# Twelve-layer decoder on one core: first keys and values of layers two and eight projected in the layers before them, statistics and transposes of layer five moved, orders of DVE in layer nine joined

## The chip, the cores and the metric

One program runs on one core of a Trainium2 chip. The core has a TensorE (PE, matrix products and transposes), a VectorE (DVE), a ScalarE (ACT), a GpSimdE (POOL) and a queue for transfers (SP), each with an instruction stream of its own. Semaphores order the streams, and what waits in a stream holds everything behind it. The metric is the device time of one execution in microseconds: 3483.48 us, the median of three runs (3479.71 to 3483.94).

## The reference

Eight sequences of 256 positions with 256 channels go through four decoder layers of three sublayers each, so twelve steps, which are here called layers one to twelve. (The code counts them from 0: layer one is `l0_attn`, named 0 in tiles and pools, and layer nine is `l2_ffn`, named 8.) After each sublayer a layer norm follows:

```python
x = _layernorm(x + _L0_attn_ref(x, ...))              # one: 16 heads of 16
x = _layernorm(x + _L0_xattn_ref(x, ctx_768, ...))    # two: one head of 256, keys from a context
x = _layernorm(x + _L0_ffn_ref(x, ...))               # three: all of 8 experts
x = _layernorm(x + _L1_attn_ref(x, ...))              # four: 16 heads, biases linear in distance
x = _layernorm(x + _L1_xattn_ref(ctx_768, x, mask_BxS2_bk0, ...))  # five: keys from both
x = _layernorm(x + _L1_ffn_ref(x, ...))               # six: 2 of 8 experts for a whole sequence
x = _layernorm(x + _L2_attn_ref(x, ...))              # seven: 16 heads, causal
x = _layernorm(x + _L2_xattn_ref(x, ctx_768, ...))    # eight: 8 heads of 64 over the context
x = _layernorm(x + _L2_ffn_ref(x, ...))               # nine: below
...                                                   # ten, eleven: 16 heads of 64; twelve: experts
```

In layer nine a shared expert (squared ReLU) works on every token. Of eight routed experts the best two by a router count with the integer part of their softmax weight, which is 0 unless one weight rounds to 1:

```python
prob = jnp.trunc(prob)
h = _sq_relu(jnp.einsum('td,edf->tef', xf, W1))
out_routed = jnp.einsum('ted,te->td', y, prob)
return (out_shared + out_routed).reshape(shape)
```

## The kernel before

All is float32. The activations of a sequence (an element, b = 0 to 7) lie in `xs[b]`, positions on partitions, and transposed in `xT`, two elements to a tile. The layers are unrolled one behind the other.

**What sets the order.** The program is written as text, and a planner lays down each engine's instructions before the run: it goes through time with a cost model and gives each engine the earliest instruction in the text that is ready by then, so work of a later layer can come before the end of an earlier one. Tiles come from pools with a number of buffers, and a tile waits for the release of the buffer that it gets. A pool's memory is free once every tile in it has been read for the last time. Weights come from a ring of six tiles (`wtile`), loads by SP; a load can go as soon as its ring tile is free. Where the planner's order is not wanted, `order_of_text` (L161) chains the instructions of the engines it names in the order of the text. Only what goes through `matmul`, `transpose`, `dve` and `pool` is chained (L149); `nc.vector`, `nc.scalar` and `nc.gpsimd` are not. `behind_latest` (L140) ties an unchained stretch behind the latest recorded instruction.

**Evacuation.** `evac` (L183) copies from PSUM by a counter, every third copy on ACT and the others on DVE. `leave` (L190) takes ACT where DVE is chained, without counting, and `evac` elsewhere.

**16-head layers** (one, four, seven; `attention16`, L390) chain PE and DVE. A block i is half the heads of an element, so block 14 and 15 are the last element. It has four steps: `step` (L466) forms scores of block i + 1 for their maxima (DVE), scores of block i, transposed and with the maxima subtracted, and their exponential (ACT). Between the steps stand the projections of the next element, the products with the values (`attend`), the normalisation (`normalise`, two reciprocals and two products on DVE), the output projection of the element before and its norm. In the last element no projections of a next one stand between the steps.

**Layer two** (`l0_xattn`, L1000) has no chain: for each element queries (`pq`), keys (`pk`), values (`pv`), scores, softmax, products and norm.

**Layers eight, ten, eleven** (`attention64`, L688) chain PE alone. Two units (pairs of heads) share a group's projections; a unit's scores, its exponentials and their transposition, and its products with the values go in a pipeline three units deep.

**Layer five** (`l1_xattn`, L1143) chains PE and DVE. For element b the four stages `front_sources`, `front_project`, `front_values`, `front_heads` run beside the four units of the element before. `front_stats` and `front_norms` precede them. The statistics of element 0 (`begin4`, L1131) are formed at the end of layer four. `finish` transposes a finished element. `choose` (L1365) finds the two experts of layer six for element 0 in the middle of layer five, 25 small DVE instructions on a path of their own.

**Layer nine** (`l2_ffn`, L1480). For each of four pairs of elements the router is computed: logits (`token_logits`, L865: product, copy `lT`, transpose, copy `L`), the best two (`top2`), softmax, gates. The last element's norm and transpose are left over from layer eight (`left`, three parts) and are worked off ahead of the fourth pair. Then the gates are summed over all tokens (`most`, `count`). A branch on the count skips the routed experts where it is 0. `expert(p, 0)` is the shared expert of pair p: product `ph`, ReLU on ACT, square on DVE, product `py`, addition. After the branch come the fourth shared expert and the norms of elements 0 and 1.

## Time and profile before

The profiled execution took 3468.22 us, of which the span is 3466.5 us. By stretches of the span (engine columns: us busy):

| stretch, us | what | length | PE | DVE | ACT | POOL | granted clock |
|---|---|---|---|---|---|---|---|
| 0 to 236 | layer one | 236 | 216.37 | 155.17 | 102.06 | 22.87 | 0.99 |
| 236 to 322 | layer two | 86 | 82.33 | 44.77 | 17.36 | 7.41 | 1.00 |
| 985 to 1216 | layer four | 231 | 214.96 | 178.19 | 67.26 | 21.05 | 0.98 |
| 1216 to 1236 | layer five, start | 20 | 14.60 | 11.74 | 7.37 | 15.64 | 0.83 |
| 1236 to 1450 | layer five, rest | 214 | 199.22 | 145.86 | 126.82 | 155.52 | 0.98 |
| 1676 to 1906 | layer seven | 230 | 203.42 | 177.60 | 83.88 | 59.31 | 0.96 |
| 1906 to 2136 | layer eight, begin of nine | 230 | 218.46 | 124.51 | 87.52 | 77.37 | 1.00 |
| 2136 to 2165 | layer nine, rest | 29 | 15.68 | 15.61 | 2.08 | 2.78 | 0.71 |

A row of the timeline gives start, duration, engine, line, operation, the tile written and those read, their shapes, and in brackets how long the engine was idle before and what ended that. Most lines of `matmul` are L178, of `transpose` L181 and of `dve` L173, so a row is known by its tiles. The granted clock is the share of full speed that TensorE got.

### The profile page before, as it was taken

Reading aid. Unit: us, or ns where it says so; the run is one execution under the profiler, and the core shown is the slowest. Engines: PE = TensorE matmul, PEld = TensorE weight load, DVE = VectorE, ACT = ScalarE, POOL = GpSimd, SP = SyncE. Lnnn points to the kernel's source line nnn. Section 1 sums busy time; section 2 is a strip of 40 time slices with the busy share of each in tenths; the row PEclk is TensorE's granted clock in tenths of the full one; section 3 lists DMA queues with packets and bytes.
Section 4 is the critical chain, followed back from the end, with each engine's and each line's share of the span. In section 5 each row is a group of like instructions: output and inputs, shape, how many; then the busy total and the mean of one; then the engine's idle time right before and its main releaser. Section 6 shows DMA issues by size and latency. Waiting matters only on the chain. (4 is left out here: it accounts for less than half of the span.)

```text
span 3466.5 us, 49726 instructions
## 1 busy us (share of the span) xinstructions
PE 3291.9 (95%) x20456; PEld 2353.2 (68%) x20456; DVE 1657.3 (48%) x3181; ACT 1057.8 (31%) x2563; POOL 849.8 (25%) x918
## 2 busy tenths in 40 slices
PE   8999999999999989999898998999998999999998
PEld 5666555655555566788666665677776766678887
DVE  5764222222358777521587555766665455530003
ACT  4432111111113355522333342433333443321111
POOL 1000000000011077522122332332223344332214
PEclk9999999999999999999999999999999999999999
DMA  3006400000000001144100101000000000025542
GB/s 107 2 10 138 173 19 19 19 19 25 22 1 1 2 13 57 55 166 156 51 2 2 49 1 56 7 1 1 1 14 30 1 13 13 13 88 190 187 147 76
DMA packets 63386, 168.35 MB, mean 49 GB/s; under 512 B 7888, under 2 KB 38353, under 8 KB 51441
## 3 DMA queue, kind: packets, MB, share of 16 engines
q1 hardware_dynamic: 47408, 76.15, 7.4%
q0 software_dynamic: 15744, 88.94, 7.2%
q8 instruction: 165, 2.70, 0.3%
q14 instruction: 69, 0.56, 0.1%
HBM read 131.78 MB, written 33.29 MB: 48 GB/s over the span
## 5 line engine op out<-in xcount | busy, mean ns | idle before, releaser
L670 POOL TENSOR_TENSOR ex<-ex,urc 128x1024 f32<-128x1024 f32 x192 | 363.4, 1894 | 615.7 <-DVE urc L173 581.4
L173 DVE TENSOR_REDUCE nm<-s 128x4 f32<-128x1024 f32 (+2 forms) x448 | 455.7, 1030 | 100.1 <-PE s L178 49.4
L661 ACT ACTIVATE ex<-s,nm 128x256 f32<-128x256 f32 (+1 forms) x704 | 337.7, 493 | 390.8 <-DVE nm L173 371.2
L515 ACT ACTIVATE eT<-t 128x1024 f32<-128x1024 f32 (+1 forms) x192 | 182.7, 953 | 353.1 <-PE t L178 353.1
L1097 DVE TENSOR_TENSOR h<-pu,sg 128x512 f32<-128x512 f32 x128 | 88.5, 691 | 331.3 <-PE pu L933 326.4
L1096 ACT ACTIVATE sg<-pg 128x512 f32<-128x512 f32 x128 | 76.3, 597 | 548.9 <-PE pg L933 548.8
L933 PE MATMUL pu<-xT_l,w2a 128*128 128x512 f32 x512 | 241.3, 593 | 0.0
L933 PE MATMUL pg<-xT_l,w2a 128*128 128x512 f32 x512 | 241.3, 593 | 0.0
L178 PE MATMUL s<-qk,qk 32*128 32x256 f32 (+1 forms) x1536 | 212.9, 393 | 25.8 <-DVE nm L173 18.8
L918 PE MATMUL py<-w2b,h 128*128 128x256 f32 x1024 | 226.2, 379 | 0.0
L918 PEld LDWEIGHTS py<-w2b,h 128*128 128x128 f32 x1024 | 195.0, 190 | 39.6 <-issue 15.3
L181 PE MATMUL etr<-ident,ex 128*128 128x128 f32 x1568 | 210.5, 277 | 7.3 <-POOL ex L670 2.4
L178 PE MATMUL t<-qm,qk 32*128 32x256 f32 (+1 forms) x1536 | 204.0, 386 | 8.5 <-DVE nm L173 7.2
L181 PEld LDWEIGHTS etr<-ident,ex 128*128 128x128 f32 x1568 | 176.6, 141 | 51.7 <-issue 34.4
L178 PE MATMUL av<-eT,vg 128*64 128x256 f32 x1536 | 204.7, 391 | 0.7 <-DVE eT L173 0.6
L178 PE MATMUL s<-kg,qg 64*128 64x256 f32 x1280 | 176.8, 395 | 26.3 <-ACT qg L732 12.1
L178 PEld LDWEIGHTS s<-qk,qk 32*128 32x128 f32 x1536 | 123.6, 187 | 92.6 <-issue 46.7
L933 PEld LDWEIGHTS pu<-xT_l,w2a 128*128 128x128 f32 x512 | 97.2, 191 | 120.7 <-issue 120.2
L933 PEld LDWEIGHTS pg<-xT_l,w2a 128*128 128x128 f32 x512 | 96.7, 190 | 106.1 <-issue 104.7
L178 PEld LDWEIGHTS s<-kg,qg 64*128 64x128 f32 x1280 | 115.2, 186 | 77.8 <-ACT qg L732 26.5
L173 DVE COPY eT<-etr 128x1024 f32<-128x1024 f32 (+1 forms) x113 | 134.6, 1191 | 57.9 <-PE etr L181 57.8
L173 POOL TENSOR_SCALAR ve_l<-mv_l 128x2 f32<-128x2 f32 x104 | 23.5, 226 | 532.2 <-DVE mv_l L173 531.4
(351 smaller groups left out, 5878.3 us busy)
## 6 DMA issues: line engine op xcount, KB each, us to landing
slots<-zero SPq DMA_DIRECT2D x16, 1024.0 KB, 13.0
given<-yo SPq DMA_DIRECT2D x19, 256.0 KB, 3.1
w2a<-in_L_ffn_Wg SPq DMA_DIRECT2D x8, 512.0 KB, 4.1
w2a<-in_L_ffn_Wu SPq DMA_DIRECT2D x8, 512.0 KB, 4.9
w2b<-in_L_ffn_Wd SPq DMA_DIRECT2D x8, 512.0 KB, 3.9
lines<-w9r SPq DMA_DIRECT2D x1, 4096.0 KB, 42.7
bias<-lines SPq DMA_DIRECT2D x4, 768.0 KB, 8.9
x<-in_x SPq DMA_DIRECT2D x8, 256.0 KB, 5.4
```

What stands on the lines that cost most here:

```text
L173: return lambda *args, **kw: in_order(getattr(getattr(nc, self.engine), op)(*args, **kw))
L178: in_order(nc.tensor.matmul(*args, **kw))
L181: in_order(nc.tensor.transpose(*args))
L515: nc.scalar.activation(eT[:, :, :n], tt[:, :, :n], AF.Exp)
L661: nc.scalar.activation(ex[:, g, :], flat[:, g, :], AF.Exp, bias=nm[:, g:g + 1], accum_out=sums[:, g:g + 1])
L670: nc.gpsimd.tensor_tensor(ex, ex, rc[:, :nseg].unsqueeze(2).to_broadcast([P, nseg, 1024 // nseg]), ALU.mult)
L918: nc.tensor.matmul(py[:, q * D:(q + 1) * D], h[:, f, i * P:(i + 1) * P], w2[:, f, :], start=(f == 0), stop=(f == nf - 1))
L933: nc.tensor.matmul(ph, w1[:, c, f * P:(f + 1) * P], xT[p][:, c, :], start=(c == 0), stop=(c == 1))
L1096: nc.scalar.activation(sg, pg, AF.Silu)
L1097: nc.vector.tensor_tensor(h[:, f, :], pu, sg, ALU.mult)
```

## The change

- Layer one loads layer two's weights in its own text (`prepare1`) and computes the keys and values of element 0 between steps 0, 1 and 2 of block 14 (`fill`), into a ring tile. Layer two takes them for element 0. The key bias of element 0 goes on ACT; the value bias is recorded in DVE's chain.
- Layer seven does the same for layer eight's first group (`begin`, `end`), evacuated by ACT.
- `at_end` (layer five's first statistics) moves from behind block 15's normalisation to behind block 14's. Element 1's statistics move behind element 0's sources. The transposes of the last two elements in layer five move to later units.
- `choose(0, 1)` in layer five leaves DVE's chain (`free_order`).
- Layer nine chains DVE. The last element's norm comes first, the logits of all pairs go into one tile, and one best-of-two over all 16 token blocks (`choose8`) replaces four. An expert is split into its two halves.
- Helpers of routers and experts record their DVE instructions, and `iota8` has one row of eight.

```diff
-    iota8 = const.tile([P, 4, E8], F32, tag="iota8", name="iota8")
-    nc.gpsimd.iota(iota8, pattern=[[0, 4], [1, E8]], base=0, channel_multiplier=0,
+    iota8 = const.tile([P, 1, E8], F32, tag="iota8", name="iota8")
+    nc.gpsimd.iota(iota8, pattern=[[0, 1], [1, E8]], base=0, channel_multiplier=0,
...
+    @contextmanager
+    def free_order(engine):
+        last = chains.pop(engine)
+        yield
+        chains[engine] = last
...
                             pk = project_qk(b + 1, 1)
+                        else:
+                            work_off(fill, 1)
                         step(i, 1)
+                        if not more:
+                            work_off(fill, 1)
...
                             pv = proj_tok(wv, xTb(b + 1), 0, f"pv_{li}_{b + 1}")
+                        elif at_end is not None:
+                            at_end()
...
-                if at_end is not None:
-                    at_end()
...
             parts = project(*units[0][:2])
-            for i in (3, 0, 1, 2):
+            if kv is not None:
+                groups[0, 0].update(k=kv[0], v=kv[1])
+            for i in (3, 0, 1, 2) if kv is None else (3,):
                 parts[i]()
...
     def top2(L, n, name):
+        for got in top2_parts(L, n, name):
+            pass
+        return got
+    def top2_parts(L, n, name, small=small):
...
+            yield vals, hots, ids
...
+    def token_logits(xTp, wr, name, pool, L=None):
...
-        nc.vector.tensor_copy(lT, pl[:, 0:P])
+        dve.tensor_copy(lT, pl[:, 0:P])
...
+            dst = L
+            if dst is None:
+                dst = small.tile([P, 2 * NT, E8], F32, tag="L", name=f"L_{name}")
+            dve.tensor_copy(dst, tr[:, 0:P].rearrange("p (i e) -> p i e", e=32)[:, :, :E8])
+            return dst
...
-    def top2_gates(p, wr, gates, name, trunc, pool):
...
-                nc.vector.tensor_tensor(xs[b], py.rearrange("p (q d) -> p q d", q=NT), xs[b],
+                dve.tensor_tensor(xs[b], py.rearrange("p (q d) -> p q d", q=NT), xs[b],
...
+        fill = []
+        if not last:
+            prepare1()
+            ready1["kv"] = first_keys(1)
+            fill = [lambda: keys1(ready1["kv"][0], 0), lambda: values1(ready1["kv"][1], 0)]
...
+                    bv=bv, bo=bo, last=last, arrive=arrive, fill=fill)
...
-    def l0_xattn(last):
+    ready1 = {}
+    def prepare1():
...
+        ready1["w"] = wq, wk_, wv, halves, bqs, bk, bv
+    def keys1(dst, b):
+        _, wk_, _, halves, _, bk, _ = ready1["w"]
+        pk = proj_T(wk_, [h[:, b * S:(b + 1) * S] for h in halves], 0, f"pk_1_{b}")
+        for c in range(2):
+            if b == 0:
+                nc.scalar.activation(dst[:, c, :], pk[:, c * S:(c + 1) * S], AF.Identity,
+                                     bias=bk[:, c:c + 1])
+            else:
+                nc.vector.tensor_scalar(dst[:, c, :], pk[:, c * S:(c + 1) * S], bk[:, c:c + 1],
+                                        None, ALU.add)
+    def values1(dst, b):
+        _, _, wv, halves, _, _, bv = ready1["w"]
+        pv = proj_tok(wv, [h[:, b * S:(b + 1) * S] for h in halves], 0, f"pv_1_{b}")
+        dve.tensor_tensor(dst, pv.rearrange("p (q d) -> p q d", q=NT),
+                          bv.unsqueeze(1).to_broadcast([P, NT, D]), ALU.add)
+    def first_keys(name):
+        w = wtile(f"kv{name}")
+        return [w[:, 512 * i:512 * i + 512].rearrange("p (c s) -> p c s", c=2) for i in range(2)]
+    def l0_xattn(last):
+        if not ready1:
+            prepare1()
+        wq, _, _, _, bqs, _, _ = ready1["w"]
...
-                pk = proj_T(wk_, kv, 0, f"pk_{nm}")
...
-                pv = proj_tok(wv, kv, 0, f"pv_{nm}")
...
+                if b == 0 and "kv" in ready1:
+                    kg, vg = ready1["kv"]
+                else:
+                    kg = wk.tile([P, 2, S], F32, tag="kg", name=f"kg_{nm}")
+                    keys1(kg, b)
+                    vg = wk.tile([P, NT, D], F32, tag="vg", name=f"vg_{nm}")
+                    values1(vg, b)
...
-                for b in range(2):
-                    if "stats" not in front.get(b, {}):
-                        front_stats(b)
+                if "stats" not in front.get(0, {}):
+                    front_stats(0)
                 front_norms(0)
                 front_sources(0)
+                front_stats(1)
                 front_norms(1)
...
-                    if j == 1 and b > 1:
+                    if b > 1 and j == (1 if b < B - 1 or last else b - B + 3):
...
                         elif j == 2:
-                            choose(0, 1)
+                            with free_order(mybir.EngineType.DVE):
+                                choose(0, 1)
...
+        fill = []
+        if not last:
+            prepare7()
+            ready7["kv"] = kg, vg = first_keys(7)
+            part = []
+            def begin():
+                part.append(project_ctx(ready7["w"][1], 0, 0, "7_0_0"))
+            def end():
+                pk, pv, rest = part.pop()
+                rest()
+                nc.scalar.copy(kg, pk.rearrange("p (c s) -> p c s", c=2))
+                nc.scalar.copy(vg, pv.rearrange("p (q d) -> p q d", q=NT))
+            fill = [begin, end]
+        attention16(6, "causal", wq, wk_, wv, wo, last=last, fill=fill)
...
+    ready7 = {}
+    def prepare7():
...
+        ready7["w"] = wq, wkv, wo, load_row("L2_xattn_bo", D)
...
+        attention64(7, 8, wq, wkv, wo, 0.125, ctx=True, bo=bo, last=last, kv=ready7.get("kv"))
...
-                nc.vector.tensor_tensor(h[:, 0, :], ph, rl, ALU.mult)
+                dve.tensor_tensor(h[:, 0, :], ph, rl, ALU.mult)
+                return h
+            def expert_ends(p, e, h):
...
-            for p in range(NB2):
-                if p == NB2 - 1:
-                    expert(0, 0)
-                    work_off(left)
-                top2_gates(p, wr, gates[:, p], f"8_{p}", True, wk)
-            expert(1, 0)
...
-            expert(2, 0)
+            def choose8(L):
+                class once:
+                    def tile(self, *args, **kw):
+                        return wk.tile(*args, **kw, bufs=1)
+                n = B * NT
+                for vals, hots, _ in top2_parts(L, n, "8", once()):
...
+                for i, pr in enumerate(softmax2(vals, n, "8", once())):
+                    c = wk.tile([P, n], F32, tag=f"cut{i}", name=f"cut{i}_8", bufs=1)
+                    dve.tensor_scalar(c, pr, 1.0, None, ALU.is_ge)
...
+                dve.tensor_tensor(flat, hots[0], bc8(cut[0], n), ALU.mult)
+                dve.tensor_tensor(g2, hots[1], bc8(cut[1], n), ALU.mult)
+                dve.tensor_tensor(flat, flat, g2, ALU.add)
...
+                dve.tensor_reduce(most, gates.rearrange("p b i e -> p (b i e)"), AX.X, ALU.add)
...
+                dve.tensor_copy(count, pc[:, 0:1])
+                yield count
+            with order_of_text(mybir.EngineType.DVE):
+                L8 = wk.tile([P, B * NT, E8], F32, tag="L8", name="L8", bufs=1)
...
+                def logits8(p):
+                    return token_logits(xT[p], wr, f"8_{p}", wk, L8[:, 2 * NT * p:2 * NT * (p + 1), :])
+                work_off(left, 1)
+                turned = [logits8(p) for p in range(2)]
+                h = expert(0, 0)
+                work_off(left, 1)
+                for f in turned:
+                    f()
+                work_off(left)
+                turned = [logits8(p) for p in (2, 3)]
+                expert_ends(0, 0, h)
+                for f in turned:
+                    f()
+                parts = choose8(L8)
+                next(parts)
+                h = expert(1, 0)
+                next(parts)
+                expert_ends(1, 0, h)
+                h = expert(2, 0)
+                count = next(parts)
+                expert_ends(2, 0, h)
             routed_ = nc.values_load(count[0:1, 0:1], min_val=0, max_val=2 * B * S)
...
+                        expert_ends(p, e, expert(p, e))
+            expert_ends(3, 0, expert(3, 0))
```

## The prediction

> **What bounds the kernel now.** The page's first part and its clock row, read first, say that TensorE bounds it: busy 95% of the span, at full clock nearly throughout. Whatever is to be won lies in the 175 us in which PE waits or in the stretches in which its clock is granted at half.
>
> ```profile
> span 3466.5 us, 49726 instructions
> PE 3291.9 (95%) x20456; PEld 2353.2 (68%) x20456; DVE 1657.3 (48%) x3181; ACT 1057.8 (31%) x2563; POOL 849.8 (25%) x918
> PEclk9999999999999999999999999999999999999999
> ```
>
> Next the table of waits, PE alone. The long single waits (last number) each occur once or a few times: at layer ends and around the two routers.
>
> ```profile
> PE lTtr L181 <- DVE z_l L173: 4.9, 2, 4.3
> ...
> PE ph L933 <- DVE x L173: 4.4, 1, 4.4
> PE ktr L181 <- ACT qT L1242: 4.2, 5, 2.8
> ...
> PE count L178 <- DVE most L1511: 4.1, 1, 4.1
> ```
>
> Then the timeline at each place, in order of time (start, duration, what, idle before). Layer one's last element has two gaps; layer two's first keys and values follow 20 us later; an element in the middle of layer five has DVE blocked and PE behind it; layer seven has an output projection at half clock, and layer eight's first scores; layer nine's end is nearly all gaps.
>
> ```profile
> 211.44 0.49 PE L178 MATMUL s<-qk,qk 32*128 32x256 f32 x2 [1.46 <-DVE nm L173]
> 213.90 0.48 PE L178 MATMUL s<-qk,qk 32*128 32x256 f32 x2 [1.31 <-DVE nm L173]
> 236.01 2.00 PE L178 MATMUL pk<-w0c,w0x 96*128 96x256 f32 x8 [0.78 <-DVE x L173]
> 237.84 1.89 PE L178 MATMUL pv<-w0x,w0c 96*128 96x256 f32 x8
> 1333.81 1.89 POOL L670 TENSOR_TENSOR ex<-ex,urc 128x1024 f32<-128x1024 f32 x1
> 1333.95 1.77 DVE L173 SCALAR_TENSOR_TENSOR tcur<-tht,L 128x8 f32<-128x8 f32 x1
> 1337.65 0.66 PE L181 MATMUL ktr<-ident,raw 128*128 128x128 f32 x4 [2.85 <-ACT qT L1242]
> 1340.82 3.78 PE L178 MATMUL po<-w4b,aT 128*128 128x256 f32 x8 [1.13 <-DVE kT L173]
> 1421.09 1.98 PE L178 MATMUL po<-w4b,aT 128*128 128x256 f32 x8
> 1883.69 3.78 PE L178 MATMUL po<-w6a,aT 128*128 128x256 f32 x8
> 1909.93 1.14 PE L178 MATMUL s<-kg,qg 64*128 64x256 f32 x8 [0.94 <-DVE kg L702]
> 2142.20 0.33 PE L181 MATMUL xtr_l<-ident,x 128*128 128x128 f32 x1 [3.49 <-DVE x L173]
> 2150.63 0.16 DVE L1515 CAST count<-count 128x1 int32<-128x1 f32 x1 [0.74 <-PE count L178]
> 2154.95 3.75 PE L933 MATMUL ph<-xT_l,w8a 128*128 128x512 f32 x4 [4.36 <-DVE x L173]
> ```
>
> Last, the busy time by stretch (length, then busy time and instructions of PE, PEld, DVE, ACT, POOL, the clock, DMA): an element of layer eight leaves PE 1.1 us idle, layer nine's end 13 of 29 us, at a clock of 0.71.
>
> ```profile
> 2014.03:2041.34 27.31, 26.20 (x165) 18.91 (x165) 14.28 (x24) 10.66 (x38) 9.73 (x7) 1.00 0.00 1
> 2136.00:2165.00 29.00, 15.68 (x64) 10.45 (x64) 15.61 (x64) 2.08 (x5) 2.78 (x6) 0.71 0.23 77
> ```
>
> **The change part by part.** Durations are of the profiled execution: span 3466.5 us, 3468.22 us in all, 15.3 us (0.44%) under the median 3483.48 of the runs shown. I sum against 3468.22 and carry the difference over to the median.
>
> *First keys and values of layer two, moved into layer one.* 16 matmuls, 2.00 + 1.89 us, leave 236 to 240 us and go between the steps at 209 to 214 us. Before each stands a wait (1.46 and 1.31 us) for the maxima on DVE, which has two reciprocals of 0.95, two products of 0.29 and a reduction of 1.23 there. So 2.77 of 3.89 us is covered, and the element ends 1.0 us later by my count; the value bias (0.69 us) now stands in DVE's fixed order before the third step's maxima, which wait for PE anyway. The two key biases go to ACT (2 x 0.42 us), which idles 1.5 us around each step. At the other end the first scores wait only for the queries, whose evacuation (0.84 us on ACT) is held by the last addition of layer one until 236.0; PE fills this with the next queries. Net: 3.6 us less there, 1.0 more here, **-2.6 us**. Ends: all 3.89 + 0.78 won (-4.7); nothing covered and the bias on the path (+0.7). The eight loads of the weights stand at 10.6 to 15.3 us on SP already, behind the x loads, and one POOL multiplication goes with them. The two tiles for ready keys and values cost a ring slot each: the first w2a load goes from 26 us to layer one's end (236), w2b from 235 to about 247 when the keys are read; landing takes 4 to 5 us, and they are needed at 321. In layer nine's ring w8c waits for 1905 and w9a for about 1927; needed after 2160. No price while these 75 and 230 us of cover stand; without it one landing, 5 us.
>
> *Layer four to five.* The statistics of element 0 (2.3 us of DVE) go to 1208, where DVE idles until 1212.3. Those of element 1 (2.3 us) go behind element 0's sources. Today both stand before z_l at 1218.75, which PE awaits for 4.32 us. Then z_l can start when the last addition frees the pool, about 1216.5, and POOL's two xb (1.26, 1.40) still beside it. What is late next is the reductions of squares: behind them in DVE's order the second statistics wait for POOL's 0.22 + 0.71, and POOL's three pairs (1.64 + 1.04) then pace the key transposes. **-2.3 us**; ends -5.0 (the whole wait and some clock) and +1.0 (that statistics pair in the way).
>
> *Router of layer six inside layer five.* Output projections of layer five's elements start at 1282.6, 1309.0, 1340.8, 1368.9, 1394.9, 1421.1: the two spans with the router's 25 small DVE instructions are 59.9 us where others give 2 x 26.1. So it costs 7.7 us today, 1.8 of it the halved clock (3.78 against 1.98). Freed from DVE's fixed order, its instructions may be interleaved with the next scores' and keys'; DVE is 67% busy in this layer, so the 4.1 us of work fits. One instruction stalls 1.6 us more, ending with POOL's multiplication. POOL's multiplications go on beside it, so I take two such stalls (3.2 us) as still paid, nearer to the row than to none: **-4.5 us**; ends -7.7 and +1.0 (the exponential on ACT waited for by other work). [...]
>
> *Late transposes of layer five.* The transpose at 1430.90 waited 1.34 us, that at 1444.08 0.34; a unit later x is ready. **-1.0**, ends -1.7 and +0.6.
>
> *Layer eight's first keys and values, into layer seven.* PE there waits 1.04 + 0.67 + 0.91 + 0.32 between 1877 and 1882, which covers 2.9 of the 3.3 us moved (1.13 + 1.03 and eight narrow matmuls, 1.1); two evacuations (0.58 each) go to idle ACT, DVE sheds 0.69. The projection at 1883.69 then probably runs at full clock (1.8 us less, of which I take 1.4). Layer eight's first scores start right after the queries' evacuation at 1905.9 instead of 1909.93: 4.0. So 0.4 - 1.4 - 4.0 = **-5.0**; ends -7.0 and 0.
>
> *Layer nine's router.* Today its last quarter waits: statistics of element 7 begin only at 2138.7, then transposes, logits and a 4.0 us top-two, count at 2150.6, and PE returns 4.3 us later. After: statistics at 2125.5 (1.2), two copies 0.6, wait and square 1.3, scaling 0.74, copies 0.4; transposes, copy, logits, copy 2.5 to 3.6; two additions 1.4; copies 0.4; eleven top-two steps on four times the width, 0.28 each between the 0.19 and 0.29 rows, 3.1; two squares and two additions 2.8; softmax with its hop to ACT, gates, sum 2.8; count 0.9. The sum gives 2143.6 to 2144.7, 6 to 7 us sooner; PE's 4.3 us after it remains. With a little of the halved clock **-7.0**; ends -11 and +3 (each fixed order meeting its wait).
>
> *Copies that alternate between DVE and ACT.* Every third goes to ACT by a counter; it falls one behind in layer eight (a copy less) and two from layer nine on (a transpose's copy goes to ACT). In layer eight nine copies make an element, so the new assignment holds for all eight. 0, ends -9 (8 x its 1.1 us idle) and +11 (8 x 1.35, below).
>
> Smaller iota and DVE-recorded helper copies: same instructions, 0.
>
> Sum -22.4: 3445.8 profiled, **3461** as the median.
>
> **The rivals.** *Port lock*: the router keeps its whole 7.7 us, since POOL's multiplications (1.89 us, four to an element of 26) stall its instructions, as at 1333.95, wherever they stand. For it: the 1.77 us row; against: one in 25 was hit. -22.4 + 4.5 = -17.9, 3466. [...] *Stalls move on*: fills mostly lengthen their elements (-2.6 and -5.0 become -1 and -3), the router saves nothing, layer nine half: -22.4 + 3.6 + 4.5 + 3.5 = -11, 3472. For: these elements are paced by DVE. *Fixed order stands in line*: DVE's one order in layer nine waits for each transposition and square, up to its bad end, and fills and router as before: -22.4 + 10 + 3.6 + 4.5 = -4, 3479. For: seven hops between PE, ACT and DVE; against: most inputs are ready long before. *Alternation, the other side*: elements of layer ten took 56.25, 57.07, 57.60 us with the same work and a rotated assignment; if each of 24 elements in layers eight, ten and eleven lost 1.35, it is +32 - 22 = +10, 3493; it decides from 1.2 each. Against: ten and eleven rotate anyway (17 copies an element), and in eight DVE's share falls from 5.7 to 5.2 us.
>
> [...]
>
> **How the numbers follow.** Forecast 0.48 (own range 3453 to 3468), port lock 0.15, stalls that move on 0.17, line 0.12, alternation 0.08. About 0.2% (7 us) can be told from no change: faster 0.80, same 0.12, slower 0.08. Low 3445 takes most of the good ends (-38), high 3480 reaches past the line case; some 0.17 stays out.
>
> **What would show it.** No wait over 0.6 us near 211 to 214; layer two's first scores and layer eight's 2 to 5 us sooner after their layers' starts; transposes lTtr waiting under 2.5 us; projections of layer five at most 29 us apart; count 6 us nearer to layer eight's end. Wrong if elements of layer eight exceed 28 us, if the count is no nearer, or if w2 loads stall layer three.

## The result, and the profile after

The changed kernel takes 3458.2 us, the median of six runs (3455.85 to 3463.13), against 3483.3 us for the kernel before; the ratio is 0.9936 with a 95% interval of 0.9925 to 0.9947. Its profiled execution took 3456.42 us, of which the span is 3454.7. The forecast was 3461, in a range of 3445 to 3480.

Kernels that ran as one set shared a chip, and the kernel before took 3468.85 us in one set and 3480 to 3485 in the others; the profile of before that the forecast used (3468.22 us) is like the first kind, the first profile of after like the second. So the fair pairs are *quiet*: the profile of before with the span 3466.5 and the second profile of after with 3445.4, -21.1 us; and *slow tail*: 3481.5 and 3454.7, -26.8 us. The forecast's sum was -22.4.

The first part of the page of the changed kernel: PE is busy for 95% as before.

```profile
span 3454.7 us, 49655 instructions
PE 3288.1 (95%) x20456; PEld 2344.7 (68%) x20456; DVE 1647.1 (48%) x3117; ACT 1059.9 (31%) x2564; POOL 849.2 (25%) x918
```

The table of PE's waits of the changed kernel (sum, times, longest). The wait for `lTtr` fell from 4.3 to 2.4 and not to nothing; `ktr` still waits 2.2 for a copy on ACT. The wait at the branch is 4.8 where it was 4.4. The wait of 4.1 for `most` is gone: it is 0.33 in the timeline below.

```profile
PE ph L937 <- PEq L1621: 4.8, 1, 4.8
...
PE lTtr L188 <- DVE z_l L180: 3.8, 3, 2.4
PE ktr L188 <- ACT qT L1279: 3.6, 5, 2.2
...
PE py L922 <- DVE h L180: 2.2, 2, 1.6
```

Rows of its timeline at the changed places, in order of time. Layer two's first keys now stand between two steps of layer one, without a wait. The first scores of layer two (`sc`) and of layer eight (`s<-kv,qg`) follow right behind their queries. `z_l` runs beside POOL's addition `xb`, and the router's `tcur` beside POOL's multiplication of the exponentials. The count comes 18 us behind layer eight's end, and PE waits for the branch.

```profile
207.53 1.99 PE L185 MATMUL pk<-w0c,w0x 96*128 96x256 f32 x8
235.54 1.89 PE L1073 MATMUL sc<-kv,qg 128*128 128x256 f32 x8
1208.82 2.68 DVE L180 TENSOR_SCALAR z_l<-x,mv_l,rs_l 128x256 f32<-128x256 f32 x2
1208.82 2.53 POOL L382 TENSOR_TENSOR xb<-x,c_L_xattn_bo 128x512 f32<-128x512 f32 x2 [5.19 <-DVE x L180]
1324.83 1.89 POOL L682 TENSOR_TENSOR ex<-ex,urc 128x1024 f32<-128x1024 f32 x1
1324.98 1.77 DVE L180 SCALAR_TENSOR_TENSOR tcur<-tht,L 128x8 f32<-128x8 f32 x1
1327.25 0.20 ACT L876 ACTIVATE s2e<-s2d 128x1 f32<-128x1 f32 x1 [3.18 <-DVE s2d L180]
1327.36 0.67 ACT L1279 ACTIVATE qT<-qtr,gq 128x512 f32<-128x512 f32 x1
1328.08 0.66 PE L188 MATMUL ktr<-ident,raw 128*128 128x128 f32 x4 [2.25 <-ACT qT L1279]
1892.28 1.14 PE L185 MATMUL s<-kv,qg 64*128 64x256 f32 x8 [0.77 <-ACT qg L745]
2125.43 0.35 PE L185 MATMUL count<-most,ones 128*128 128x1 f32 x2 [0.33 <-DVE most L180]
2130.60 3.75 PE L937 MATMUL ph<-xT_l,w8a 128*128 128x512 f32 x4 [4.81 <-PEq L1621]
```

Busy time by stretch (columns as in the forecast's): an element of layer eight, which takes 27.10 us where it took 27.31, and all from layer eight's end to layer ten's first scores, first in the changed kernel and then in the kernel before. The granted clock there is 0.91 in place of 0.80.

```profile
2006.30:2033.40 27.10, 26.21 (x166) 18.87 (x164) 13.73 (x23) 10.99 (x37) 9.74 (x8) 1.00 0.00 1
2107.43:2143.45 36.02, 27.21 (x155) 17.29 (x154) 20.98 (x63) 4.28 (x8) 2.98 (x7) 0.91 0.36 119
```

```profile
2124.78:2167.82 43.04, 29.72 (x155) 19.05 (x155) 26.22 (x124) 4.38 (x10) 2.98 (x7) 0.80 0.29 96
```

**Where the time came from.** Length of each layer in us, from the last or first PE instruction of its kind to the next layer's. "Halved" is PE's busy time inside stretches of half clock, divided by two: what those stretches cost at most. The four columns are the two fair pairs.

| stretch | before (3466.5) | after (3445.4) | before (3481.5) | after (3454.7) |
|---|---|---|---|---|
| layer one, first 30 us | 30.00 (halved 1.71) | 30.00 | 30.00 | 30.00 |
| layer one, rest | 205.23 | 203.84 | 202.79 | 203.79 |
| layer two | 82.55 | 78.48 | 82.55 | 78.46 |
| layer three | 672.40 | 673.00 | 672.41 | 672.99 |
| layer four | 225.38 (4.67) | 222.75 (1.71) | 224.00 (3.40) | 222.71 (1.71) |
| layer five, start | 22.56 (2.70) | 21.36 (2.79) | 22.98 (3.74) | 21.40 (2.75) |
| layer five, rest | 211.50 (2.85) | 207.44 | 210.71 (2.79) | 207.35 |
| layer six | 224.56 | 225.00 | 224.56 | 225.00 |
| layer seven | 230.98 (8.29) | 229.37 (6.83) | 230.40 (7.78) | 229.81 (8.01) |
| layer eight | 219.62 | 216.01 | 219.63 | 215.92 |
| layer nine to count | 25.81 (1.02) | 18.35 | 25.84 (1.05) | 18.35 |
| count to first scores of ten | 17.23 (3.09) | 17.70 (2.30) | 17.47 (2.58) | 17.67 (2.30) |
| layer ten | 457.11 | 455.43 (1.71) | 457.12 | 455.43 (1.71) |
| layer eleven | 439.26 | 444.78 (5.07) | 445.66 (1.71) | 446.13 (3.35) |
| layer twelve | 402.33 (1.71) | 401.92 (1.52) | 415.40 (6.46) | 409.68 (3.39) |

The lengths from layer two to layer ten agree between the pairs to 1.4 us, so the gains sit where the change was made; the ends of the program do not agree, and the experiments say what that goes with.

### The profile page after: what moved, and what is told of

Same layout as the page of the kernel before. It is cut to its first block, busy times and chain, and to the rows that moved or that the text cites. A ratio compares the mean times of both kernels' runs of the same rounds, so it can differ in the third digit from the quotient of the medians.

```text
span 3454.7 us, 49655 instructions
## 1 busy us (share of the span) xinstructions
PE 3288.1 (95%) x20456; PEld 2344.7 (68%) x20456; DVE 1647.1 (48%) x3117; ACT 1059.9 (31%) x2564; POOL 849.2 (25%) x918
```

## The experiments

Two kinds of evidence are used: the time, by its ratio to the kernel before in the same set (intervals of 0.09 to 0.15% to each side, 3 to 5 us), and the trace, in which each PE instruction is matched with the same one of the other kernel's trace, so that a change of a microsecond is seen at its place.

### The changed kernel again

No edit.

> The changed kernel once more. In the first profile its half-clock stretches begin at 995.5, 1210.6, 1667.9, 1685.0, 1702.1, 1862.5, 2128.7, 2582.7, 2862.6, 3033.3, 3074.2 and 3391.7 us, all a whole number of 3.413 us apart, as those of the kernel before are among themselves. Theory grid: the clock is set anew every 3.413 us on a grid whose start differs from execution to execution, and a gap of 2 us halves it only where most of it falls into one window. Then long gaps (1210, 2129) halve it again, and the five from 2583 on, behind gaps of 2.0 to 2.5 us, come and go: about half of them missing, 2 us each. Rival, fixed: the stretches belong to the kernel and stand at the same gaps again, all five. Time 3455 to 3463 by both.

Measured: 3448.94 us, ratio 0.9947 (0.9932 to 0.9962). The stretches of half clock behind the gaps at 1210 and 2129 came back, as did those at 2582.7, 2862.6, 3033.3 and (one window on) 3077.7; those at 1862.5 and 3391.7 did not, and one at 1756.7 and one at 2613.5 were new. So of the five from 2583 on four stayed, more than the grid theory had expected: this profile's grid happened to begin only 0.016 us from the first one's. Over all 14 profiles of this study the grid holds: in each of them every stretch starts a whole number of 3.413 us from every other (within 7 ns), and the grid's start against the first instruction lies anywhere between 0.13 and 2.9 us. What goes with the halving is the idle time of PE inside one such window, summed over its gaps, more than one long gap: of the 56 windows in the last row six have no gap over 1.61 us, and of 49 windows with a longer gap than that, but under 1.9 us of idling in all, 4 were followed by half clock. Windows at full clock (without the first two and the last few of each profile), and how often the next one was halved:

| idle in the window, us | windows | next one halved |
|---|---|---|
| under 0.6 | 12678 | 0 |
| 0.6 to 1.2 | 813 | 12 |
| 1.2 to 1.9 | 285 | 53 |
| 1.9 to 2.1 | 35 | 27 |
| 2.1 and more | 56 | 56 |

Between 0.6 and 1.9 us, 55 of the 65 halvings stand in layers one, four and seven, whose score matmuls have 32 rows. So something beside idle time counts there; what it is, is not shown.

### Without the two moved projections

```diff
         fill = []
-        if not last:
+        if False:
             prepare1()
...
         fill = []
-        if not last:
+        if False:
             prepare7()
```

> The changed kernel without the two moved projections (both fill lists empty, so layers two and eight project their first keys and values themselves, as before). Theory sum (each part is worth what its place in the two traces shows): 3.1 us lost at layer two's begin and 4.1 at layer eight's, perhaps 1.5 more of halved clock at layer seven's end: 7 to 9 us slower than the changed kernel, 3465 to 3467. Rival, elsewhere (the loads moved and the ring places cost as much as the fills win): within 2 us of 3458. A second rival, copies: with one copy more counted in layer eight the alternation of DVE and ACT goes back by one there, and elements of layer eight take 0.2 us longer each, of ten and eleven some other length.

Measured: 3458.05 us, ratio 0.9971 (0.9962 to 0.9980), 9.1 us slower than the changed kernel in the same set (0.9947). Its timeline has the projections back ahead of the first scores of layer two:

```profile
233.54 1.99 PE L185 MATMUL pk<-w0c,w0x 96*128 96x256 f32 x8 [0.78 <-DVE x L180]
235.37 1.89 PE L185 MATMUL pv<-w0x,w0c 96*128 96x256 f32 x8
237.10 1.89 PE L1073 MATMUL sc<-kg,qg 128*128 128x256 f32 x8
...
1874.83 3.78 PE L185 MATMUL po<-w6a,aT 128*128 128x256 f32 x8
```

Against the changed kernel the trace gains 0.93 us in layer one's last element, loses 4.07 at layer two's begin, 2.9 at layer seven's end and 5.2 at layer eight's begin (5.73 less 0.57). The last two hold halved clock: the output projection takes 3.78 us again. A stretch of 6.8 us of half clock stands here in all three profiles without this fill and in none of the eleven with it (at most 3.4 us). "Sum" holds, "elsewhere" is out. The rival "copies" shows in the trace as well: elements of layer eight take 27.30 us where the changed kernel has 27.10, and layer ten takes 457.68 us where it has 455.43. So some 2 us of the loss are the counter's and not the fills'.

### Layer six's router back in DVE's order

```diff
-                            with free_order(mybir.EngineType.DVE):
-                                choose(0, 1)
+                            choose(0, 1)
```

> The changed kernel with the router of layer six kept in DVE's fixed order in layer five. Theory order: the element with the router lasts 31.8 us between output projections as in the kernel before, against 30.1 after; the other half of the 3.9 us that the two traces differ by there was the clock, at half for 6.8 us in one of them, so the loss is 1.7 us, and 3.9 where the clock is halved. Rival, order and clock are one: 3.9 us at any rate, the clock being halved by the longer gap (2.85 against 2.25 us). Rival, port: no difference at all, since the instruction that lasts 1.77 us beside POOL's multiplication and the exponential on ACT behind it hold up the key transposes in both. Time 3458 to 3462.

Measured: 3449.44 us, ratio 0.9945 (0.9931 to 0.9959): the time can't tell it from the changed kernel. The trace can. The projections around the router start 31.83 and 28.14 us apart, 59.97 together; in the changed kernel 30.10 and 25.93, together 56.03. So the fixed order costs 3.9 us: 1.7 in the router's own element and 2.2 in the next, by half clock. That is the rival "order and clock are one": all three profiles with the router in the order have 6.8 us of half clock at this place, and none of the eleven others has any.

```profile
1328.63 1.78 DVE L180 SCALAR_TENSOR_TENSOR tcur<-tht,L 128x8 f32<-128x8 f32 x1
...
1332.34 0.66 PE L188 MATMUL ktr<-ident,raw 128*128 128x128 f32 x4 [2.86 <-ACT qT L1279]
```

`tcur` takes 1.78 us here too. The freed order shortened the wait behind it from 2.86 to 2.25 us and no more.

### POOL's multiplications beside the router left out

```diff
                     if n < len(units):
-                        unit_scale(exs[n])
+                        unit_scale(exs[n], times=n // 4 != 3)
...
+        if times:
             nc.gpsimd.tensor_tensor(
```

> The changed kernel in which POOL's four multiplications of the exponentials by the reciprocal sums are left out for the fourth element of layer five (so that element's attention is not normalised), the element beside which layer six's router runs. Theory port: the router's instruction tcur, 1.77 us in three profiles and ending with POOL's multiplication each time, falls to 0.17 to 0.19 us; the exponential of its softmax, which waits for it on ACT, and the query copy queued behind that come 1.6 us sooner, and PE's wait of 2.25 us for the key transposes falls to about 0.7; output projections there 28.3 to 28.6 us apart instead of 30.1. Rival, order: tcur is long because of its place in the order, not because of POOL: still 1.7 us. Rival, cover: tcur is short, but the element stays at 30 us since something else holds the query copy.

Measured: of this kernel only layer five is compared, since the fourth element's attention is another and the experts of later layers get other work with it (3529.1 us in all). These are the rows of the changed kernel's `tcur`, `s2e`, `qT` and `ktr` without the multiplications:

```profile
1328.07 0.17 DVE L180 SCALAR_TENSOR_TENSOR tcur<-tht,L 128x8 f32<-128x8 f32 x1
...
1328.74 0.20 ACT L877 ACTIVATE s2e<-s2d 128x1 f32<-128x1 f32 x1 [1.59 <-DVE s2d L180]
1328.85 0.67 ACT L1280 ACTIVATE qT<-qtr,gq 128x512 f32<-128x512 f32 x1
...
1329.58 0.66 PE L188 MATMUL ktr<-ident,raw 128*128 128x128 f32 x4 [0.65 <-ACT qT L1280]
```

`tcur` falls from 1.77 to 0.17 us, ACT's wait from 3.18 to 1.59, PE's from 2.25 to 0.65, and the projections stand 28.51 us apart. The theory "port" holds in every number: without POOL's multiplication the stall is gone, and each following wait is shorter by the same 1.6 us. Why `tcur` lasts until the multiplication ends (both at 1326.7 in the changed kernel) no row shows. The element is still longer than its neighbours (26.46 and 25.92 us): PE has 0.8 us more of work in it, and waits of 0.69, 0.65 and 0.51 us.

### The router's softmax two steps later

```diff
-                                choose(0, 1)
+                                weigh = choose(0, 1)
...
+                    if n == 16 and not last:
+                        weigh()
```

(`choose` returns its softmax part as a function, and the rows for the fetch are formed at once.)

> The changed kernel with the softmax of layer six's router (nothing needs it before layer six) recorded two steps after its top-two. Theory ACT queue: what is left of the router's price in layer five is the query copy standing on ACT behind the softmax's exponential; with that gone the wait of 2.25 us for the key transposes falls under 0.6 and the projections stand 27.5 to 28.5 us apart instead of 30.1, though tcur still lasts 1.77 us. 2 us faster than the changed kernel. Rival, DVE: the 1.77 us stall itself holds DVE's scores and maxima up, so the spacing stays at 29.5 to 30.1.

Measured: 3461.79 us, ratio 0.9936 (0.9922 to 0.9949); projections 30.09 us apart, as in the changed kernel. The wait for `ktr` falls to 0.34 us, and the next one, for `kT`, is 2.42 us:

```profile
1328.86 1.79 DVE L180 SCALAR_TENSOR_TENSOR tcur<-tht,L 128x8 f32<-128x8 f32 x1
...
1330.05 0.66 PE L188 MATMUL ktr<-ident,raw 128*128 128x128 f32 x4 [0.34 <-ACT qT L1279]
...
1333.99 1.99 PE L185 MATMUL po<-w4b,aT 128*128 128x256 f32 x8 [2.42 <-DVE kT L180]
```

In the changed kernel that one is short:

```profile
1330.15 1.99 PE L185 MATMUL po<-w4b,aT 128*128 128x256 f32 x8 [0.55 <-DVE kT L180]
```

My theory of the ACT queue fell, the rival DVE was right. The query copy on ACT was one of two ways from the stalled instruction to PE; with it cleared, the scores and maxima on DVE, 1.6 us late as well, hold up the key copy `kT`.

### Layer nine as before

```diff
-            with order_of_text(mybir.EngineType.DVE):
-                L8 = wk.tile([P, B * NT, E8], F32, tag="L8", name="L8", bufs=1)
...
+            for p in range(NB2):
+                if p == NB2 - 1:
+                    expert(0, 0)
+                    work_off(left)
+                top2_gates(p, wr, gates[:, p], f"8_{p}", True, wk)
+            expert(1, 0)
```

> The changed kernel with layer nine as before (four routers, no fixed order on DVE). Theory sum: count comes 7.0 us later against the end of layer eight, and all behind it with it: 3465. Rival, copies: layer nine's part changes which copies go to ACT in layers ten and eleven, and the 48 half elements there differ by 0.3 to 1.5 us up and down in the two traces; then the difference in time is not 7 but anything from 4 to 10, and the surplus stands in layers ten and eleven. Rival, clock: a good part of the 7.0 is the 17 us of half clock before against 6.8 after, so with the count back where it was the half clock returns too and the loss is the 7 us, but only 3 to 4 of it in waits.

Measured: 3453.53 us, ratio 0.9959 (0.9945 to 0.9973), 4.6 us slower than the changed kernel by the medians, though the intervals overlap. In the trace the count comes 5.9 us later behind layer eight's end (24.28 against 18.35) and layer ten's first scores 7.5 later (43.55 against 36.05); 23.9 us of half clock stand there against 6.8.

```profile
2135.35 0.56 PE L185 MATMUL count<-most,ones 128*128 128x1 f32 x2 [3.79 <-DVE most L1590]
```

Some of the 7.5 us is given back: layers eleven and twelve are 4.8 and 1.3 us shorter than in the changed kernel's trace of that set, with 3.4 and 1.5 us less of halved clock in them, while layer ten is 1.0 us longer. The count is 5.9 us later and not 7.0, so "sum" holds but for 1.1 us; the kernel before has its count another 1.5 us later (25.81), and why is not shown. The rival "clock" holds too: by the measure of the table above, halved clock costs at most 7.2 us here and at most 2.3 in the changed kernel, so up to 4.9 of the 7.5 us can be clock.

### Statistics and late transposes of layer five as before

```diff
-                        elif at_end is not None:
-                            at_end()
...
+                if at_end is not None:
+                    at_end()
...
-                    if b > 1 and j == (1 if b < B - 1 or last else b - B + 3):
+                    if j == 1 and b > 1:
```

(and both elements' statistics ahead of `front_norms(0)`)

> The changed kernel with the statistics of layer five's first two elements and its last transposes where they were before. Theory sum: PE waits 4.3 instead of 2.4 us for lTtr, and with what comes later the start of layer five is 1.1 to 1.5 us longer (21.4 to 22.6 us between layer four's last projection and layer five's first scores); the late transposes gave nothing (0.4 us the other way). So about 1 us slower than the changed kernel, 0 to 2, within the scatter of the time. Rival, the forecast's sizes: 2.3 + 1.0 = 3.3 us slower. Rival, clock: the 2.8 us lost around 1190 in the kernel before, where PE's clock was at half, come back too, since the statistics stood in the way of DVE there: 4 us slower.

Measured: 3467.6 us, ratio 0.9944 (0.9930 to 0.9958), not to be told from the changed kernel's 0.9936. The wait for `lTtr` is 4.32 us again and the start of layer five 22.99 us, 1.6 longer than 21.36:

```profile
1213.66 1.30 DVE L180 TENSOR_SCALAR z_l<-x,mv_l,rs_l 128x256 f32<-128x256 f32 x2
1214.79 0.89 PE L188 MATMUL lTtr<-ident,z_l 128*128 128x128 f32 x4 [4.32 <-DVE z_l L180]
```

The old transposes gave 0.41 us back behind 1440, so the new ones win nothing there. At the places that they left, the changed kernel's PE waits for ACT's `eT` instead:

```profile
1417.82 1.13 PE L185 MATMUL s<-kT,qT 64*128 64x512 f32 x4 [1.10 <-ACT eT L200]
...
1431.97 1.95 PE L185 MATMUL av<-eT,vg 128*64 128x256 f32 x16 [1.10 <-ACT eT L200]
```
Layer five's rest was 2.7 us longer with two stretches of half clock (at 1249.5 and 1423.5), which neither profile of before has. Nothing came back at 1190, so the rival "clock" is out: the half clock there in one profile of before was that grid's, and three later profiles with the moved statistics have it too (at 1190.3 to 1193.3).

### The counter of the copies

```diff
+            if li == 7:
+                turn[0] += 1
...
+            turn[0] += 1
             for b in range(2):
                 norm_and_transpose(b, xs[b], "l8", last)
```

> The changed kernel with one added to the copies' counter at layer eight's begin and one behind layer nine, so that the copies fall on DVE and ACT in layers eight, ten and eleven just as in the kernel before; all else stays. Theory alternation: layer ten gets its 464.6 us again (461.2 in the changed kernel), layer eleven its 439.3 (441.9 to 446.1, of which 1.7 to 5.1 are halved clock behind gaps of over 2 us), layer eight 0.4 us less: in all 1 us slower to 3 faster than the changed kernel. Rival, other causes: layers ten and eleven keep their 461 and 442 to 446 us, the difference having come with the later events of layer nine.

Measured: 3461.98 us, ratio 0.9944 (0.9930 to 0.9957). The copies fall as in the kernel before in all three layers, and layer eight stays at 215.97 us (216.01 in the changed kernel). Layer ten, from its first scores on, takes 457.17 us as in the kernel before (457.11 and 457.12) and not 455.43, which eight profiles with the changed kernel's start have within 0.06 us. So the counter alone is worth 1.7 us there, about half of what the theory had from first queries on. Layer eleven has 444.50 us without any halved clock, where the kernel before has 439.26 in one set and 445.66 in the other; the next experiment shows that this is not the counter.

### The kernel before again

No edit.

> The kernel before once more, with a profile. Its earlier profile lasted 3466.5 us, the changed kernel's two 3454.7 and 3445.4. Profiles that lasted long have 5 to 10 us in layer twelve around 3380 to 3400, where ACT starts on a product's columns 8.6 instead of 2.0 us after the product began and nothing shown ends its wait, and 4 to 5 us more in layer eleven. Theory chip: this goes with the chip or the hour, not with the kernel; where the kernel before takes about 3484 us its own profile has these delays as well (layer eleven 444 instead of 439.3 us, layer twelve 406 to 415 instead of 402.3), and where it takes 3469 us it has none. Rival, kernel: the delays belong to the changed kernel and its like, and the kernel before has 439 and 402 us in any case.

Measured: 3479.95 us, ratio 1.0000 (0.9989 to 1.0011). Layer eleven takes 445.66 us and layer twelve 415.40, so the theory holds: these delays go with the set and not with the kernel. In layer twelve ACT starts 8.5 us behind a product's begin, and its next step 2.8 us behind that:

```profile
3405.22 7.07 PE L1776 MATMUL ph_s<-xT_l,w11a_s 128*128 128x256 f32 x32
3413.71 0.60 ACT L1778 ACTIVATE h_s<-ph_s 128x512 f32<-128x512 f32 x1 [14.60 <-PE ph_s L1776]
3416.54 0.60 ACT L1778 ACTIVATE h_s<-ph_s 128x512 f32<-128x512 f32 x1 [2.23 <-remote]
```

The same place in the changed kernel's second profile, in the quiet set, has 2.0 and 1.7 us:

```profile
3378.80 7.07 PE L1879 MATMUL ph_s<-xT_l,w11a_s 128*128 128x256 f32 x32
3380.79 0.60 ACT L1881 ACTIVATE h_s<-ph_s 128x512 f32<-128x512 f32 x1 [8.10 <-PE ph_s L1879]
3382.46 0.60 ACT L1881 ACTIVATE h_s<-ph_s 128x512 f32<-128x512 f32 x1 [1.07 <-PE ph_s L1879]
```

ACT takes the product in four parts. The bracket names PE's product as what ended its wait, and the trace has the semaphore that PE raises behind each part at 3413.63, 3416.52, 3419.38 and 3422.21; by its row, whose end is modelled, the first part was done at 3407.11. So it is PE that was late and not ACT that was held. What made PE late no row shows; it stays open. This delay explains the first comparison, in which the changed kernel's profile lost 14 us in its last two layers: one profile was from a quiet set, the other not.

### ACT for the colliding multiplication, and half an expert ahead of the branch

```diff
-                        unit_scale(exs[n])
+                        unit_scale(exs[n], on_act=n == 14)
...
+                h = expert(3, 0)
             routed_ = nc.values_load(count[0:1, 0:1], min_val=0, max_val=2 * B * S)
...
-            expert_ends(3, 0, expert(3, 0))
+            expert_ends(3, 0, h)
```

> The changed kernel with two additions. In layer five the one multiplication of POOL that coincides with the router's tcur is done by ACT in two parts (0.7 us each); in layer nine the first half of the fourth shared expert (product, ReLU, square) stands ahead of the branch, its second half behind it. Theory: tcur falls to 0.17 to 0.19 us and the projections there to 28.5 to 29 us apart (30.1); in layer nine PE waits about 1 to 3 us at the branch instead of 4.8 and layer ten's first queries start 2 to 3 us sooner behind the count (12.2 us in the changed kernel): 3 to 5 us faster than the changed kernel, a ratio of 0.993 to 0.9925 where the changed kernel has 0.9936 to 0.9947. Rival, moved wait: the branch lets go at the same time, and the norms of the first two elements behind it, some 5 us of DVE and POOL that the fourth expert covered, now stand open: no gain in layer nine. Rival, ACT: the two multiplications stand on ACT ahead of the exponential and the query copy: no gain in layer five.

Measured: 3461.52 us, ratio 0.9951 (0.9938 to 0.9965). In layer five `tcur` takes 0.17 us, the wait for `ktr` is 0.65 and the projections stand 28.67 us apart: that part holds. In layer nine PE waits as long as before:

```profile
2131.43 0.35 PE L185 MATMUL count<-most,ones 128*128 128x1 f32 x2 [0.33 <-DVE most L180]
2131.83 0.16 DVE L180 CAST count<-count 128x1 int32<-128x1 f32 x1 [0.54 <-PE count L185]
...
2136.39 3.75 PE L926 MATMUL py<-w8a,h 128*128 128x256 f32 x8 [4.60 <-DVEq L1627]
```

The view of the branch's line has each engine's branch instruction (least, median and most ns):

```profile
L1627 ACTq COMPARE_BRANCH  x1: 50/50/50, 2132.5 to 2132.5; - x1
...
L1627 PEldq COMPARE_BRANCH  x1: 3342/3342/3342, 2132.6 to 2132.6; - x1
L1627 DVEq COMPARE_BRANCH  x1: 72/72/72, 2132.6 to 2132.6; - x1
```

The branch lets PE go 4.4 us after the count's cast ends, and 4.6 in the changed kernel (2125.98 to 2130.60). Most of that is PE's own branch instruction, 3.34 us here and 3.81 there. The product that I moved ahead of it ran before the count, in a gap of PE, and the count came no sooner. The rival "moved wait" is right in that nothing is gained: layer ten's first scores come 20.1 us behind the count where they came 17.7. That the move itself costs 2.4 us is not shown, since more of the stretch is at half clock (5.38 us against 2.30), and the nine profiles with the changed kernel's layer nine have 17.1 to 19.6 us there, with 1.42 to 4.46 us halved.

### The third start of the counter

```diff
+            if li == 7:
+                turn[0] += 2
...
+            turn[0] -= 1
             for b in range(2):
                 norm_and_transpose(b, xs[b], "l8", last)
```

> The same kernel with the third of the three possible starts of the copies' counter in layers eight, ten and eleven. Theory: the alternation moves little (under 1.5 us in any of the three layers, as between the other two starts, 216.0 and 216.0 in layer eight, 473.1 and 474.2 from count to layer ten's end). Rival: this start is the bad one or the good one, 8 x 1.1 to 1.35 us in layer eight alone, as the ends of the forecast had it.

Measured: 3461.31 us, ratio 0.9946 (0.9933 to 0.9960). Layer eight takes 211.83 us, 4.1 less than the other two starts and 3.9 less than the kernel of the last experiment (215.69), from which only the counter differs. These are one element of it in the changed kernel (its second profile) and in this one, from one output projection to the next:

```profile
1988.80:2015.90 27.10, 26.20 (x167) 18.88 (x165) 13.74 (x24) 11.01 (x38) 9.74 (x7) 1.00 0.01 2
```

```profile
2017.90:2044.50 26.60, 26.11 (x166) 18.87 (x164) 14.38 (x24) 10.70 (x38) 9.74 (x7) 1.00 0.00 1
```

DVE does more here, and the element is 0.50 us shorter: which copy waits decides, not whose share is larger. In the changed kernel PE waits 1.55 us in the layer for transposes copied by ACT and 4.7 for queries; here nothing and 3.3. Half of the rival was right: this start is the good one, by 4.1 us and not by 9. Layer ten lost it again (459.40 us against 455.43, 3.41 of it halved).

### Both gains without the loss

```diff
+            if li == 7:
+                turn[0] += 2
...
-                        unit_scale(exs[n])
+                        unit_scale(exs[n], on_act=n == 14)
...
+            turn[0] -= 2
             for b in range(2):
                 norm_and_transpose(b, xs[b], "l8", last)
```

> The changed kernel with POOL's one multiplication beside the router's tcur done by ACT, the copies' counter two further in layer eight, and back where the changed kernel has it for layers ten and eleven; layer nine as in the changed kernel. Theory sum: layer eight 211.8 us as with the third start (215.9 to 216.0 in the changed kernel), layer five's rest 206.2 to 206.4 (207.4), count to layer ten's end 473.1 as there: 5.3 us faster than the changed kernel, a ratio to the kernel before of 0.992 to 0.993 where the changed kernel had 0.9936 and 0.9947. Rival, given back: what layer eight wins is lost in the layers ten to twelve, by halved clock or another alternation, as with the third start there (468.3 us for layer ten): the ratio stays at 0.9936 to 0.995.

Measured: 3457.3 us, ratio 0.9928 (0.9914 to 0.9941). The parts are there: layer eight 211.78 us, layer five's rest 206.25, 5.3 less than in the changed kernel. Of that the time shows little: this is the lowest ratio of all, but its interval overlaps the changed kernel's. Its profile lost 5 us in layer four, at a place that nothing had touched: half clock for 10.2 us at 996.8 and for 6.8 at 1191.4, where the changed kernel has 3.4 and none. Another 1.9 went between the count and layer ten's first scores (4.46 halved there against 2.30).

## Why the prediction was right, and where it was not

The time, the sign and the sum were right: -22.4 us forecast, -21.1 and -26.8 in the fair pairs, 3461 forecast and 3458.2 measured. By the medians the change is worth 25.1 us in the first set and 19.9 in the quiet one. That the quiet pair comes so near is in part luck: beside the steps below, layer one without its fill (-2.3), layer three (+0.6), four (-2.6), eleven (+5.5) and twelve (-0.4) changed as well, mostly with the halved clock, and cancel to 0.8 us. By steps, in us (the trace column is the quiet pair, the last the difference that undoing it makes in the trace):

| step | forecast | trace | undone |
|---|---|---|---|
| fill of layer one | -2.6 | -3.1 | 3.1 |
| layer four to five | -2.3 | -1.2 | 1.6 |
| router in layer five | -4.5 | -3.9 | 3.9 |
| late transposes | -1.0 | +0.4 | -0.4 |
| fill of layer seven | -5.0 | -5.2 | 8.1 with halved clock |
| layer nine | -7.0 | -7.0 to layer ten's first scores | 7.5 |
| copies' counter | 0 | -1.7 in layer ten | 0.0 in layer eight, 1.7 in ten |

- *Fill of layer one.* The last element grew by 0.93 us where I had counted 1.0, and layer two's begin shrank by 4.07 where I had 3.6. The waits of 1.46 and 1.31 us are gone, and no load of layer three came late: no wait over 0.3 us stands at its begin, though the layer is 0.6 us longer. It is so without the fills too (673.17 us), so they are not the cause, which stays open.
- *Layer four to five.* Mis-sized, by the cover that I had named as harmless. I let `z_l` start "about 1216.5, and POOL's two xb still beside it". It did start 0.9 us behind the last projection's end, with POOL's `xb` at the same instant, and its two instructions took 1.35 and 1.42 us where a pair with no `xb` beside it takes 0.79 (at 1217.92 in the kernel with the statistics as before). So 1.9 of the 4.3 us that I freed went, by my estimate, to a collision with POOL like the router's. No run here takes it away; it rests on these rows.
- *Router.* The size was right, the account not. I took the fixed order as the cost and two stalls of 1.6 us as still paid. One stall was still paid, and it alone carries 1.6 us through ACT and DVE to PE (the kernels without the multiplication and with the late softmax show it). The order was worth 1.7 us, and the clock that the longer gap halved another 2.2. The rival "port lock" was right about 1.6 of the 3.8 us that remain, which are gone where POOL does not multiply, but not about the size: it had the full 7.7 us remain. The rest, as the kernel without the multiplications shows, is PE's work for the router and three waits of 0.5 to 0.7 us.
- *Late transposes.* Wrong: -1.0 forecast, 0.4 the other way. They had stood where PE would else wait for ACT's `eT`; with them gone it waits 1.10 us there two times, and layer six is 0.44 us longer.
- *Fill of layer seven.* The first scores 4.0 us sooner: 4.01 measured, from layer seven's last projection. The projection at full clock: 1.99 us where 3.78 stood, in every profile with the fill.
- *Layer nine.* The count came 7.46 us sooner (6 to 7 forecast); PE's wait behind it stayed, 4.8 where I had 4.3, and 0.5 us went again up to layer ten's first scores. At most 1.8 of the 7.0 us are halved clock. Size and mechanism were right.
- *Alternation.* Taken as 0; it was 0.0 in layer eight and -1.7 in layer ten, a term of the sum that I had missed. The third start is worth 4.1 us more in layer eight, inside my bound of 9. The bound on the bad side (11) was not met by any of the three.

"Stalls move on" and "fixed order stands in line" are out as wholes: the fills paid in full, and layer nine's count came as reckoned. Elements of layer eight stayed under 28 us, as the forecast asked. The clause that layer five's projections stand at most 29 us apart failed, at 30.1, and it pointed to the collision.

## What to carry to other kernels

One DVE instruction of layer five took 1.77 us beside a multiplication on POOL and 0.17 without it, and the 1.6 us between them reached PE through two queues, ACT's and DVE's: the projections stood 30.10 us apart and 28.67 with that multiplication on ACT. So look for DVE instructions that end together with a POOL one, and try that one POOL instruction on ACT before moving the victim. Idling of PE was paid twice in these profiles where 2.1 us and more of it fell together inside 3.413 us, the second time as halved clock (56 windows of 56): filling the waits at layer seven's end took its output projection from 3.78 to 1.99 us as well. So where PE bounds, look whether filling a wait is worth more than the wait. Compare profiles only where the untouched layers agree, and read a gain of 0.1% at its place in the trace, since the time can't show it.

## What the runs showed of the hardware that was not expected

- Half clock went with the idle time of PE summed inside a window of 3.413 us: it followed none of the 12678 windows with under 0.6 us of idling, all 56 with 2.1 us and more, and 92 of the 1133 between, where idle time alone did not decide. Where the grid fell differed from execution to execution (0.13 to 2.9 us behind the first instruction), and halved stretches cost at most 19 to 33 us in each of the 14 profiles, of 12 kernels.
- Beside POOL's two `xb` (2.53 us from 1208.82 on), `z_l` took 1.35 and 1.42 us an instruction in the changed kernel; its next pair, at 1216.12 with no `xb` beside it, took 0.73 us for both.
- PE's first instruction behind the branch started 4.2 to 4.8 us after the count's cast ended in all 14 profiles. PE's own branch instruction took 3.3 to 4.0 us of it; on the other engines the branch took 0.04 to 0.07 us, and in the kernel before DVE worked on 1.3 us after the cast.
- In the second profile of the kernel before PE raised its semaphore for the first part of a product in layer twelve 6.5 us after the end that its row has, and ACT began 8.5 us behind the product's begin where it was 2.0 in the changed kernel's second profile; layers eleven and twelve were 6.4 and 13.1 us longer in that profile of the kernel before than in the other.
